# Another order of the block products in a fast matrix product on one core

## The chip, the cores and the metric

The kernel runs on one core of a Trainium2 chip. The metric is the time of the whole kernel on the device, in microseconds (us), as the median of several runs. One execution was also profiled; instructions in it are timed in nanoseconds.

## The reference

The input x has 8 batches of 512 rows of 1024 numbers, all in float32. The reference is a transformer layer with a normalization before and after each half:

```python
x = x + layernorm(attention(layernorm(x)))     # Wq, Wk, Wv, Wo, 16 heads of 64, rotary, causal
x = x + layernorm(ffn(layernorm(x)))           # x @ weight.T + bias, plus a LoRA term of rank 16
```

The LoRA term is `(x @ A.T) @ B.T`, with one of three adapters by batch. What matters here are the three products of the normalized rows with a 1024x1024 matrix: by Wv (the values), by Wo (the output projection) and by the weight of the FFN.

## The kernel before

Each of these products is made by a Strassen-Winograd scheme, twice over: seven products in place of eight at the outer level (`GROUPS`, P1 to P7), and each of these again by seven at the inner level (`SUBS`). So one batch takes 7 x 7 = 49 inner products. A batch in one of the three matrices is a **sequence**; sequences are numbered -8 to -1 for Wv (the projection stage), 0 to 7 for Wo (the output stage) and 8 to 15 for the FFN. Between the projection and the output stage lies the stage of Wq, Wk and the attention, which has a structure of its own and is not changed.

The order of all work is written out by hand. Time is counted in **ticks**: a tick is one inner product on TensorE (PE), two matmuls of 128x128 by 128x256, which in float32 are four passes in the trace. A sequence has 49 ticks, `N2`; its groups follow the list `ORDER`, and in a group the seven inner products follow `SLOTS`: P6, P1, P3, P5, P4, P7, P2. P3 in that list belongs to the group before, so that its sum can be read in two steps. `at(tick, fn)` puts a piece of work of another engine, or a DMA, to a tick, `run` issues a tick's work after its matmuls, and each engine and the DMA queue of SP take their work in the order in which it was issued. So an engine that is late delays all that is queued behind.

**Inner sums.** `product` adds the inner products in PSUM under four names, a, b, c and d. The drains (`drain`, one tick after their product) read them: after P1 ScalarE (ACT) copies a into p1 and VectorE (DVE) makes u2 = p1 + b; after P7 DVE makes p1 + b, then the quarter p1 + c (1, 1), then p1 + d (1, 0); after P2 ACT copies a, after P3 DVE makes u2 + c. A sum's bank can't be written before its last reader has read it: P3 adds to the c sum that the drain of P7 has just read.

**Outer sums.** A group's four quarters form a tile in SBUF: A, c11, c21, c22, U or c12 by group; A holds P1 and later P3. The result blocks are sums of such tiles. `COMBINE` lists them with their ticks and engines: on DVE one operation of 128x1024, on GpSimd (POOL) two of 128x512. With the order of before, the result blocks are finished by seven combines, most of them at ticks 45 to 52, the last three ticks in the next sequence. In the last sequence (15) the order was already `LAST`, with combines of its own.

**Operands.** The right operands are blocks R11, R21, R12, R22 of the rows and the sums T1 = R12 - R11, T2 = R22 - T1, T4 = R21 - T2, T3 = R22 - R12 (in R12's place). P1 uses R11, P2 R21, P3 R22, P4 T4, P5 T1, P6 T2, P7 T3. They are made during the sequence before (T1 from tick 38, T2 from 45, T4 from 52, T3 from 63, where ticks over 48 lie in the sequence that uses them), by DVE and POOL in the projection and FFN, by POOL alone in the output stage (line 275). They live in seven buffers, which change hands by `next_roles`: a block is loaded into the buffer whose group is done. The left operands (weights and their sums) stay for a whole stage; `plan_left` loads those of the FFN one by one during sequences 7 and 8.

**Other work in the same queues.** In the projection, DVE makes the statistics of the next batch (line 400), ACT normalizes it (420), PE transposes it (454). In the output and FFN stages the finished rows of a sequence are treated from tick 55 on in four parts: statistics on DVE, normalization on ACT, addition of the input on POOL (1124), and in the output stage statistics and a transposition on DVE again (1133), with loads and stores on SP.

The PSUM of the projection stage held one bank for a, two for b, two for c, one for d and two for transposes; from the output stage on a has two. That is all eight.

Of the kernel before, what the change touches and what calls it, by code (L numbers as in the profile page):

```python
# [58 lines left out]
    "P7": ("S3", "T3", "c12"),  # L59
}  # L60

ORDER = ["P1", "P2", "P4", "P5", "P7", "P6", "P3"]
LAST = ["P1", "P6", "P5", "P7", "P2", "P4", "P3"]
SUB = 256


# [12 lines left out]
ACCS = {"a": 1, "b": 2, "c": 2, "d": 1}  # L79
# [54 lines left out]
def sandwich_kernel(  # L134
# [139 lines left out]
        for c in (slice(0, 2), slice(2, 4), slice(4, 7))[part]:  # L274
            eng.tensor_tensor(RX[q, n][:, c], RX[q, x][:, c], RX[q, y][:, c], op=ALU.subtract)  # L275

    def next_roles():

        old = dict(role)
        for new, was in (("R11", "R11"), ("R21", "R21"), ("R12", "T4"), ("R22", "T1"),  # L280
                         ("T1", "R12"), ("T2", "T2"), ("T4", "R22")):
            role[new] = old[was]

    def open_c(q, tag):
# [10 lines left out]
    class Group:  # L295
# [9 lines left out]
        def product(self, p):  # L305
            l, r, a = SUBS[p]
            first = a not in self.acc
            if first:
                self.acc[a] = env["acc"].tile(
                    [P, SUB], F32, tag=a, bufs=2 if a == "a" and self.q >= 0 else ACCS[a], name=f"acc{a}_{self.name}"  # L310
                )
            acc = self.acc[a]
            left, right = self.W[self.L], RX[self.q, self.R][:, SLOT_R[r]]
            for k in range(2):
                stays = right[:, k, :] if self.q < B else by_blocks(right, k)
                if self.q < 0:
# [3 lines left out]
                nc.tensor.matmul(  # L320
                    acc, lhsT=stays, rhs=moving,
                    start=(first and k == 0), stop=True, skip_group_check=True,
                )
# [15 lines left out]
        def drain(self, p):  # L339

            acc, t = self.acc, self.t
            add = lambda out, x, a: nc.vector.tensor_tensor(out, acc[a], x, op=ALU.add)
            if p == "P1":
                env["u2"].reverse()
                for n, pool in (("p1", env["p1"]), ("u2", env["u2"][0])):
                    t[n] = pool.tile([P, SUB], F32, tag=n, name=f"{n}_{self.name}")
                nc.scalar.copy(t["p1"], acc["a"])
                add(t["u2"], t["p1"], "b")
            elif p == "P7":
                add(t["p1"], t["p1"], "b")  # L350
                add(self.dest(1, 1), t["p1"], "c")
                add(self.dest(1, 0), t["p1"], "d")
            elif p == "P2":
                nc.scalar.copy(self.dest(0, 0), acc["a"])
            elif p == "P3":
                add(self.dest(0, 1), t["u2"], "c")

    def combine(q, out, x, y, eng):
# [1 line left out]
            eng.tensor_tensor(C[q, out][:, j], C[q, x][:, j], C[q, y][:, j], op=ALU.add)  # L360


    COMBINE = (
        (18, nc.vector, "c11", "c11", "A"), (38, nc.gpsimd, "c21", "c21", "c12"),
        (45, nc.vector, "U", "U", "A"), (46, nc.vector, "c22", "c22", "U"),
        (47, nc.gpsimd, "c21", "c21", "U"), (48, nc.vector, "c12", "c12", "c22"),
        (52, nc.vector, "c22", "c22", "A"),
    )

    def products(q0, count, order, first=0):  # L370

# [100 lines left out]

    def plan_x(b, base):

        at(base + 10, next_roles)
        for t in range(NT):
            at(max(0, base - 12) + t, lambda t=t: load_x(b, t))
            k = (4, 5, 17, 19)[t]
            for m in range(4):
                at(base + k + m, lambda t=t, m=m: stats_x(b, t, m))  # L480
            at(base + k + 4, lambda t=t: norm_x(b, t))
        for n, k in (("R11", 11), ("R21", 18), ("R12", 25), ("R22", 32)):
            g, h = int(n[1]) - 1, int(n[2]) - 1
            for c in range(2):
                t = 2 * h + c
                at(base + k + c, lambda t=t, g=g: transpose_x(b, t, g), "pe")
                at(base + k + c, lambda pt, t=t, g=g: keep_x(b, t, g, pt), "post")
            at(base + k + 3, lambda n=n: sub_right(b - B, n, pool))
        for n, k in (("T1", 38), ("T2", 45), ("T4", 52), ("T3", 63)):
            eng = dve if n in ("T1", "T3") else pool  # L490
            for m in range(3):
                at(
                    base + k + (m if eng is dve else 0),
                    lambda n=n, m=m, eng=eng: sum_right(gvp, b - B, n, eng, slice(m, m + 1)),
                )
        for n, k in (
            ("R11", 18), ("R21", 25), ("R22", 40), ("T1", 44), ("T2", 54), ("T4", 60), ("T3", 69)
        ):
            at(base + k, lambda n=n: store_operand(b, n))

# [41 lines left out]
    for b in range(B):  # L542
        base = b * N2
        if b + 1 < B:
            plan_x(b + 1, base)
        for k, *op in COMBINE:
            at(base + k, lambda b=b, op=op: combine(b - B, *op[1:], op[0]))
        for k, tag, half, h in ((22, "c11", 0, 0), (53, "c21", 1, 0), (54, "c12", 1, 1), (57, "c22", 0, 1)):
            at(base + k, lambda b=b, tag=tag, half=half, h=h: store_v(b, tag, half, h))


# [337 lines left out]
    products(-B, B, lambda q: ORDER)  # L889
    psum.close()  # L890
    operands.close()
    late = {k - (B * N2 + 4): events[k] for k in sorted(events)}
# [88 lines left out]
    def first_product(n):  # L981
        nonlocal cur, before
        m, p = divmod(n, NP)
        if p == 0:
            L, R, tag = GROUPS[ORDER[m]]

            def mm(acc, p, first):
                l, r, _ = PRODUCTS[p]
                for k in range(2):
                    nc.tensor.matmul(  # L990
                        acc, lhsT=RX[0, R][:, SLOT_R[r], k, :],
                        rhs=LW["wo"][L][:, 4 * k : 4 * k + 4, SLOT_L[l], :],
                        start=(first and k == 0), stop=True, skip_group_check=True,
                    )

            def dest(i, j):
                if (0, tag) not in C:
                    open_c(0, tag)
                return C[0, tag][:, j, ts(i, SUB)]

            before, cur = cur, Product(nc, ps_p, tl, [P, SUB], f"0_{ORDER[m]}", mm, dest)
        cur.product(p)
        if p:
            cur.drain(p)
# [3 lines left out]
    for u in range(UQ + 1):  # L1008
# [15 lines left out]
        else:  # L1024
# [19 lines left out]
            at(base + 57, next_roles)  # L1044
# [21 lines left out]
    with ExitStack() as a:  # L1066
# [37 lines left out]

        def halves(q, t):
            h, j = divmod(t, 2)
            tags = (("c11", "c21"), ("c12", "c22") if q + 1 == NQ else ("c22", "c12"))[h]
            return [C[q, tag][:, j, :] for tag in tags]

        row = {}  # L1110
# [56 lines left out]
        def plan_right(q, base):  # L1167

            if q > 1:
                at(base + 6, next_roles)  # L1170
# [96 lines left out]
        for q in range(NQ):  # L1267
# [2 lines left out]
                plan_right(q + 1, base)  # L1270
            if q == B - 1:
                plan_left(base)
            dve, pool = nc.vector, nc.gpsimd
            for k, e, res, l, r in (
                (18, dve, "c11", "c11", "A"), (38, pool, "c21", "c21", "c12"), (45, dve, "U", "U", "A"),
                (46, dve, "c22", "c22", "U"), (47, pool, "c21", "c21", "U"),
                (48, dve, "c12", "c12", "c22"), (52, dve, "c22", "c22", "A"),
            ) if q + 1 < NQ else (
                (18, dve, "U", "U", "A"), (31, dve, "c12", "c12", "U"), (33, dve, "U", "U", "c22"),
                (34, pool, "c22", "c22", "c12"), (39, pool, "c11", "c11", "A"),  # L1280
                (45, dve, "c21", "c21", "c12"),
            ):
# [6 lines left out]
        products(0, NQ, lambda q: ORDER if q + 1 < NQ else LAST, AHEAD)  # L1289
        run_rest()  # L1290
    for pool in (wop2, tl, cl, gp, wop):
        pool.release()
# [105 lines left out]
```

## Time and profile before

| | us |
|---|---|
| median of 3 runs | 2468.2 (2465.58 to 2468.6) |
| profiled execution | 2470.53 |
| its span in the trace | 2468.4 |
| TensorE busy | 2356.1 (95%) |
| VectorE busy | 1790.1 (73%) |
| GpSimd busy | 1535.8 (62%) |

The first matmul of the projection starts 13 us after the start of the span, the last ends at about 429; the output stage proper begins at 1676, the FFN at 2024, and the last matmul ends at 2455. Lines of groups and waits name an engine, an operation or tile, the source line and, behind an arrow, what was read or what ended a wait. A wait is idle time of an engine between two of its instructions; three numbers behind it are the total, the count and the longest. The timeline has start, duration, engine, line, operation, out<-in and count; in brackets stands the idle time before it and who ended it.

### The profile page before, as it was taken

Reading aid. Unit: us, or ns where it says so; the run is one execution under the profiler, and the core shown is the slowest. Engines: PE = TensorE matmul, PEld = TensorE weight load, DVE = VectorE, ACT = ScalarE, POOL = GpSimd, SP = SyncE. Lnnn points to the kernel's source line nnn. Section 1 sums busy time; section 2 is a strip of 40 time slices with the busy share of each in tenths; the row PEclk is TensorE's granted clock in tenths of the full one; section 3 lists DMA queues with packets and bytes.
Section 4 is the critical chain, followed back from the end, with each engine's and each line's share of the span. In section 5 each row is a group of like instructions: output and inputs, shape, how many; then the busy total and the mean of one; then the engine's idle time right before and its main releaser. Section 6 shows DMA issues by size and latency. Waiting matters only on the chain.

```text
span 2468.4 us, 37185 instructions
## 1 busy us (share of the span) xinstructions
PE 2356.1 (95%) x11936; PEld 1858.0 (75%) x11936; DVE 1790.1 (73%) x3946; ACT 1045.4 (42%) x2650; POOL 1535.8 (62%) x1139
## 2 busy tenths in 40 slices
PE   6999999999999999999999999899999988999997
PEld 4887887886677777777777776558888867888886
DVE  8777767485857759577595866776899888776676
ACT  3323331025555555555555566652434433222223
POOL 4878875204363553735646364776887886777874
PEclk8999999999999999999999999899999999999999
DMA  7697787998899897989889897467777788545443
GB/s 264 196 302 247 245 269 230 353 304 265 269 298 291 248 340 239 312 297 292 314 259 341 265 303 245 135 230 261 241 213 233 216 261 246 136 144 148 139 122 119
DMA packets 506016, 606.47 MB, mean 246 GB/s; under 512 B 197600, under 2 KB 344032, under 8 KB 503264
## 3 DMA queue, kind: packets, MB, share of 16 engines
q1 hardware_dynamic: 504288, 598.87, 76.7%
q0 software_dynamic: 1536, 5.24, 0.7%
q8 instruction: 96, 1.57, 0.3%
q14 instruction: 96, 0.79, 0.1%
HBM read 371.20 MB, written 199.23 MB: 231 GB/s over the span
## 4 chain that ended last, share of the span: by engine, by line
PE 65%; DVE 6%; DMA 5%; POOL 2%; ACT 2%; issue 1%; SPq 1%; ACTq 0%; DVEq 0%; POOLq 0%
PE accb_q_P L641 7%; PE acca_q_P L641 7%; PE accc_q_P L641 7%; PE accc_P L320 6%; PE accb_P L320 6%; PE acca_P L320 6%; PE s L753 6%; PE po L835 6%; PE ptp L814 5%; PE accd_q_P L641 3%; PE accd_P L320 3%; DMA wo_d<-wc_wo 1%; DVE U L360 1%; ACT pr L784 1%; DMA attn<-opt 1%
## 5 line engine op out<-in xcount | busy, mean ns | idle before, releaser
L784 ACT ACTIVATE pr<-pr,nm 128x128 f32<-128x128 f32 (+3 forms) x512 | 281.0, 550 | 188.4 <-DVE nm L774 188.2
L800 ACT ACTIVATE pr<-pr,rs 128x128 f32<-128x128 f32 x470 | 231.0, 550 | 109.4 <-DVE rs L792 109.3
L774 DVE CUSTOM_DVE_ANT_0 pr<-s,mask 128x128 f32<-128x128 f32 (+3 forms) x512 | 224.2, 484 | 43.1 <-PE s L753 41.1
L641 PE MATMUL acca_q_P<-xs,ls 128*128 128x256 f32 x896 | 217.3, 385 | 0.8 <-DMA ls<-wqk 0.8
L641 PE MATMUL accc_q_P<-xs,ls 128*128 128x256 f32 x896 | 217.1, 385 | 0.0
L641 PE MATMUL accb_q_P<-xs,ls 128*128 128x256 f32 x896 | 216.3, 384 | 0.8 <-DVE u_q_P L117 0.8
L1124 POOL TENSOR_TENSOR c<-c,row 128x512 f32<-128x512 f32 x120 | 161.8, 1357 | 88.4 <-ACT c L420 73.2
L641 PEld LDWEIGHTS acca_q_P<-xs,ls 128*128 128x128 f32 x896 | 165.3, 190 | 49.9 <-issue 19.4
L641 PEld LDWEIGHTS accc_q_P<-xs,ls 128*128 128x128 f32 x896 | 165.3, 190 | 48.2 <-issue 20.2
L641 PEld LDWEIGHTS accb_q_P<-xs,ls 128*128 128x128 f32 x896 | 165.4, 190 | 44.9 <-issue 6.6
L753 PE MATMUL s<-qk 64*128 64x128 f32 (+3 forms) x1024 | 192.5, 472 | 4.4 <-DVE nm L774 4.2
L814 PE MATMUL ptp<-ident,pr 128*128 128x128 f32 x1280 | 178.7, 278 | 12.8 <-DVE nm L774 5.9
L814 PEld LDWEIGHTS ptp<-ident,pr 128*128 128x128 f32 x1280 | 147.6, 142 | 44.8 <-ACT pr L800 15.9
L275 POOL TENSOR_TENSOR T<-R,T 128x512 f32<-128x512 f32 (+1 forms) x96 | 171.3, 1812 | 14.2 <-PE accc_P L320 9.6
L567 POOL TENSOR_TENSOR wc_g<-wc_g 128x256 f32<-128x256 f32 (+1 forms) x120 | 127.0, 1077 | 79.6 <-DMA wc_g<-in_wqk_dram 76.3
L835 PE MATMUL po<-pT,v 128*64 128x512 f32 (+3 forms) x1024 | 157.6, 446 | 8.2 <-ACT pT L829 6.1
L835 PEld LDWEIGHTS po<-pT,v 128*64 128x64 f32 x1024 | 72.8, 138 | 100.1 <-issue 66.2
L684 POOL TENSOR_TENSOR B_q<-B_q,m 128x1024 f32<-128x1024 f32 x14 | 33.1, 2368 | 175.7 <-DVE B_q L681 175.7
L641 PE MATMUL accd_q_P<-xs,ls 128*128 128x256 f32 x448 | 108.8, 386 | 0.4 <-DVE p_q_P L117 0.4
L829 DVE COPY pT<-ptp 128x384 f32<-128x384 f32 (+1 forms) x132 | 80.4, 614 | 39.3 <-PE ptp L814 39.2
L753 PEld LDWEIGHTS s<-qk 64*128 64x128 f32 x1024 | 73.1, 186 | 44.7 <-issue 28.7
L567 POOL TENSOR_TENSOR wc_wo<-wc_wo 128x256 f32<-128x256 f32 (+1 forms) x64 | 66.0, 1049 | 64.2 <-DMA wc_wo<-in_wo_dram 50.8
(1120 smaller groups left out, 5750.6 us busy)
## 6 DMA issues: line engine op xcount, KB each, us to landing
ls<-wqk SPq DMA_DIRECT2D x392, 256.0 KB, 5.3
xs<-xop SPq DMA_DIRECT2D x392, 256.0 KB, 5.4
R<-attn SPq DMA_DIRECT2D x32, 896.0 KB, 6.4
wqk<-wc_g SPq DMA_DIRECT2D x16, 1568.0 KB, 9.4
x<-in_x_dram SPq DMA_DIRECT2D x32, 512.0 KB, 9.7
v<-vd SPq DMA_DIRECT2D x64, 256.0 KB, 5.4
attn<-ops SPq DMA_DIRECT2D x16, 1024.0 KB, 7.7
row<-in_x_dram SPq DMA_DIRECT2D x32, 512.0 KB, 5.4
```

Source lines behind the costliest of these rows:

```text
L275: eng.tensor_tensor(RX[q, n][:, c], RX[q, x][:, c], RX[q, y][:, c], op=ALU.subtract)
L320: nc.tensor.matmul(acc, lhsT=stays, rhs=moving, start=(first and k == 0), stop=True, skip_group_check=True,)
L567: eng.tensor_tensor(out, x, y, op=op)
L641: nc.tensor.matmul(acc[:, :, w, :], lhsT=ls[:, k, w, :], rhs=xs_[:, :, k, :], start=(first and w == 0 and k == 0), stop=True, skip_group_c ...
L753: nc.tensor.matmul(ps[:, j, at : at + L], lhsT=qT[r, qb], rhs=kT[r, : qb + 1], start=True, stop=True,)
L774: nc.vector.tensor_tensor_reduce(out=v[:, j, :], in0=self.ps[qb][:, j, :], in1=work2["mask"][:, S - L :], scale=-1.0 / HD**0.5, scalar=3.0e38,
L784: nc.scalar.activation(v[:, j, :], v[:, j, :], AF.Exp, bias=nm[:, j : j + 1], scale=-1.0, accum_out=sm[:, j : j + 1],)
L800: nc.scalar.mul(v, v, rs[:, j : j + 1])
L814: nc.tensor.transpose(pt[:, n, :], self.pr[qb][:, j, ts(kb, P)], ident)
L829: copy(self.pT[j][:, : qb + 1, ts(qb, P)], self.pt[j][:, : qb + 1, :])
L835: nc.tensor.matmul(po[j * HD : (j + 1) * HD, kb * P :], lhsT=self.v[:, kb, ts(j, HD)], rhs=self.pT[j][:, kb, kb * P :], start=(kb == 0), s ...
L1124: nc.gpsimd.tensor_tensor(c, c, row[q, t][:, ts(h, HALF)], op=ALU.add)
```

## The change

All sequences but the first of a stage (-8 and 0) take their groups in the order P1, P6, P5, P7, P2, P4, P3, which only the last sequence had before. With this order a result tile is summed soon after each group, so the combines stand at ticks 17, 31, 35, 36, 39, 45 and 52. The last one writes c12 from A and U, so the second half of the output takes its two tiles in the other order (`halves`). As the operands come free in another order, `next_roles` has a second table, and the loads of the FFN's weights follow the groups. T3 of the projection is made at tick 59 in place of 63, and the stores of the values (`store_v`) and of T3 move to where these are ready.

In PSUM the c and d sums become two halves of one bank, in two banks by turns, and a gets two banks in all stages. The quarter that reads d is now made before the one that reads c.

```diff
-ORDER = ["P1", "P2", "P4", "P5", "P7", "P6", "P3"]
-LAST = ["P1", "P6", "P5", "P7", "P2", "P4", "P3"]
+FIRST = ["P1", "P2", "P4", "P5", "P7", "P6", "P3"]
+ORDER = ["P1", "P6", "P5", "P7", "P2", "P4", "P3"]
...
-    def next_roles():
+    def next_roles(q):
...
-        for new, was in (("R11", "R11"), ("R21", "R21"), ("R12", "T4"), ("R22", "T1"),
-                         ("T1", "R12"), ("T2", "T2"), ("T4", "R22")):
+        for new, was in (
+            ("R11", "R11"), ("R21", "R21"), ("R12", "T4"), ("R22", "T1"), ("T1", "R12"), ("T2", "T2"), ("T4", "R22"),
+        ) if q - 1 in (-B, 0) else (
+            ("R11", "R11"), ("R21", "T2"), ("R12", "T1"), ("R22", "R12"), ("T1", "R21"), ("T2", "T4"), ("T4", "R22"),
+        ):
...
-            if first:
-                self.acc[a] = env["acc"].tile(
-                    [P, SUB], F32, tag=a, bufs=2 if a == "a" and self.q >= 0 else ACCS[a], name=f"acc{a}_{self.name}"
-                )
+            if a in "ab" and first:
+                self.acc[a] = env["acc"].tile([P, SUB], F32, tag=a, bufs=2, name=f"acc{a}_{self.name}")
+            elif a == "c" and first:
+                both = env["acc"].tile([P, 2, SUB], F32, tag="c", bufs=2, name=f"accc_{self.name}")
+                self.acc["c"], self.acc["d"] = both[:, 0], both[:, 1]
...
                 add(t["p1"], t["p1"], "b")
+                add(self.dest(1, 0), t["p1"], "d")
                 add(self.dest(1, 1), t["p1"], "c")
-                add(self.dest(1, 0), t["p1"], "d")
...
-    COMBINE = (
-        (18, nc.vector, "c11", "c11", "A"), (38, nc.gpsimd, "c21", "c21", "c12"),
-        (45, nc.vector, "U", "U", "A"), (46, nc.vector, "c22", "c22", "U"),
-        (47, nc.gpsimd, "c21", "c21", "U"), (48, nc.vector, "c12", "c12", "c22"),
-        (52, nc.vector, "c22", "c22", "A"),
-    )
+        first = (
+            (17, dve, "U", "U", "A"), (31, dve, "c12", "c12", "U"), (35, dve, "U", "U", "c22"),
+            (36, pool, "c22", "c22", "c12"), (39, pool, "c11", "c11", "A"), (45, dve, "c21", "c21", "c12"),
+        )
+        return first if last else (*first, (52, dve, "c12", "A", "U"))
...
-        for n, k in (("T1", 38), ("T2", 45), ("T4", 52), ("T3", 63)):
+        for n, k in (("T1", 38), ("T2", 45), ("T4", 52), ("T3", 59)):
...
-        for k, tag, half, h in ((22, "c11", 0, 0), (53, "c21", 1, 0), (54, "c12", 1, 1), (57, "c22", 0, 1)):
+        for k, tag, half, h in (
+            (41, "c22", 1, 1), (44, "c11", 0, 0), (48, "c21", 1, 0), (55, "c12", 0, 1),
+        ) if b else (
+            (22, "c11", 0, 0), (53, "c21", 1, 0), (54, "c12", 1, 1), (57, "c22", 0, 1),
+        ):
...
-            for n, k in zip(("L11", "L12", "L22", "S1", "S3", "S2", "S4"), (10, 22, 34, 46, 56, 64, 72)):
+            for n, k in zip(("L11", "S2", "S1", "S3", "L12", "L22", "S4"), (10, 22, 34, 46, 56, 64, 72)):
```

More of the change, by code (lines that the diff above doesn't have):

```diff
@@ L78 @@
 QK = {"P1": "A", "P2": "B", "P6": "D", "P7": "E", "P4": "F", "P5": "D", "P3": "E"}
-ACCS = {"a": 1, "b": 2, "c": 2, "d": 1}
 SLOT_L = {"L11": 0, "L12": 1, "S3": 2, "L22": 3, "S1": 4, "S2": 5, "S4": 6}
@@ L360, in combine, with order_of, combines @@
             eng.tensor_tensor(C[q, out][:, j], C[q, x][:, j], C[q, y][:, j], op=ALU.add)
-    COMBINE = (
-        (18, nc.vector, "c11", "c11", "A"), (38, nc.gpsimd, "c21", "c21", "c12"),
-        (45, nc.vector, "U", "U", "A"), (46, nc.vector, "c22", "c22", "U"),
-        (47, nc.gpsimd, "c21", "c21", "U"), (48, nc.vector, "c12", "c12", "c22"),
-        (52, nc.vector, "c22", "c22", "A"),
-    )
+    def order_of(q):
+        return FIRST if q in (-B, 0) else ORDER
+    def combines(q, last=False):
+        dve, pool = nc.vector, nc.gpsimd
+        if q in (-B, 0):
+            return (
+                (18, dve, "c11", "c11", "A"), (38, pool, "c21", "c21", "c12"), (45, dve, "U", "U", "A"),
+                (46, dve, "c22", "c22", "U"), (47, pool, "c21", "c21", "U"),
+                (48, dve, "c12", "c12", "c22"), (52, dve, "c22", "c22", "A"),
+            )
+        first = (
+            (17, dve, "U", "U", "A"), (31, dve, "c12", "c12", "U"), (35, dve, "U", "U", "c22"),
+            (36, pool, "c22", "c22", "c12"), (39, pool, "c11", "c11", "A"), (45, dve, "c21", "c21", "c12"),
+        )
+        return first if last else (*first, (52, dve, "c12", "A", "U"))
     def products(q0, count, order, first=0):
@@ L473, in plan_x @@
     def plan_x(b, base):
-        at(base + 10, next_roles)
+        at(base + 10, lambda: next_roles(b - B))
         for t in range(NT):
@@ L496, in plan_x @@
         for n, k in (
-            ("R11", 18), ("R21", 25), ("R22", 40), ("T1", 44), ("T2", 54), ("T4", 60), ("T3", 69)
+            ("R11", 18), ("R21", 25), ("R22", 40), ("T1", 44), ("T2", 54), ("T4", 60), ("T3", 67)
         ):
@@ L545, in sandwich_kernel @@
             plan_x(b + 1, base)
-        for k, *op in COMBINE:
+        for k, *op in combines(b - B):
             at(base + k, lambda b=b, op=op: combine(b - B, *op[1:], op[0]))
-        for k, tag, half, h in ((22, "c11", 0, 0), (53, "c21", 1, 0), (54, "c12", 1, 1), (57, "c22", 0, 1)):
+        for k, tag, half, h in (
[3 more added lines that the diff above has]
+        ):
             at(base + k, lambda b=b, tag=tag, half=half, h=h: store_v(b, tag, half, h))
@@ L887, in plan @@
                     at(base + last + k, lambda m=m: self.sum(m))
-    products(-B, B, lambda q: ORDER)
+    products(-B, B, order_of)
     psum.close()
@@ L984, in first_product @@
         if p == 0:
-            L, R, tag = GROUPS[ORDER[m]]
+            L, R, tag = GROUPS[FIRST[m]]
             def mm(acc, p, first):
@@ L999, in dest @@
                 return C[0, tag][:, j, ts(i, SUB)]
-            before, cur = cur, Product(nc, ps_p, tl, [P, SUB], f"0_{ORDER[m]}", mm, dest)
+            before, cur = cur, Product(nc, ps_p, tl, [P, SUB], f"0_{FIRST[m]}", mm, dest)
         cur.product(p)
@@ L1043, in sandwich_kernel @@
                     at(base + k + m, lambda n=n, m=m: sum_right(gp, 0, n, nc.gpsimd, slice(m, m + 1)))
-            at(base + 57, next_roles)
+            at(base + 57, lambda: next_roles(1))
             for n in ("R12", "R11", "R21"):
@@ L1106, in halves @@
             h, j = divmod(t, 2)
-            tags = (("c11", "c21"), ("c12", "c22") if q + 1 == NQ else ("c22", "c12"))[h]
+            tags = (("c11", "c21"), ("c12", "c22") if q else ("c22", "c12"))[h]
             return [C[q, tag][:, j, :] for tag in tags]
@@ L1169, in plan_right @@
             if q > 1:
-                at(base + 6, next_roles)
+                at(base + 6, lambda: next_roles(q))
             for n, k in (("R11", 10), ("R21", 17), ("R12", 24), ("R22", 31)):
@@ L1272, in sandwich_kernel @@
                 plan_left(base)
[L1273 to L1282, printed above, removed]
+            for k, e, res, l, r in combines(q, q + 1 == NQ):
                 if base + k >= AHEAD:
@@ L1288, in sandwich_kernel @@
                 plan_last(q, base)
-        products(0, NQ, lambda q: ORDER if q + 1 < NQ else LAST, AHEAD)
+        products(0, NQ, order_of, AHEAD)
         run_rest()
```

## The prediction

> **What bounds the kernel now.** I read the page first, then the waits of PE stage by stage, then the timelines of DVE and POOL around the longest of them. The page:
>
> ```profile
> span 2468.4 us, 37185 instructions
> PE 2356.1 (95%) x11936; PEld 1858.0 (75%) x11936; DVE 1790.1 (73%) x3946; ACT 1045.4 (42%) x2650; POOL 1535.8 (62%) x1139
> ```
>
> TensorE sets the time and the change leaves its matmuls alone, so only its waits can be won. One tick is four 128x256 matmul passes at 0.216 us from start to start, 0.865 us; 49 ticks are 42.4 us. A pass lasts 0.38 us and overlaps the next, so a wait costs its idle time plus 0.16 us. From first matmul to first matmul in the timeline, projection sequences -6 to -2 take 49.1 us each (46.3 without their waits; transposes are the rest), output sequences 2 to 6 take 46.2, 44.7, 44.4, 44.6 and 46.2, and FFN sequences 10 to 14 take 51.7. PE's waits in three windows (134 to 380, 1700 to 1976, 1976 to 2100 us):
>
> ```profile
> PE ptx L454 <- ACT x L420: 3.7, 15, 0.4
> PE acca_-6_P L320 <- ACT A_-6_1100 L354: 0.8, 1, 0.8
> ...
> PE accc_-4_P L320 <- DVE A_-4_2162 L342: 0.3, 1, 0.3
> ...
> PE accc_P L320 <- DVE A L342: 11.0, 6, 1.9
> PE accb_P L320 <- POOL T L275: 1.6, 1, 1.6
> ...
> PE accc_P L320 <- DVE A L342: 7.6, 2, 4.2
> PE ph L1153 <- DMA R<-x1t: 5.0, 4, 2.2
> PE accb_P L320 <- DVE u_P L342: 3.7, 2, 2.1
> ```
>
> From 2100 to 2452 us there are none. The usual wait is P3 of a sequence's last group (tick 51) for DVE's read of its c sum. Why DVE is late there, in the timeline of DVE at the seam of output sequences 3 and 4 (start, us, line, tiles):
>
> ```profile
> 1833.49 1.76 DVE L360 TENSOR_TENSOR U<-U,A 128x1024 f32<-128x1024 f32 x1
> 1835.28 2.17 DVE L360 TENSOR_TENSOR c<-c,U 128x1024 f32<-128x1024 f32 x1
> 1837.38 0.41 DVE L342 TENSOR_TENSOR p_P<-accb_P,p_P 128x256 f32<-128x256 f32 x1
> 1837.82 0.42 DVE L342 TENSOR_TENSOR A<-accc_P,p_P 128x256 f32<-128x256 f32 x1
> 1838.16 0.41 DVE L342 TENSOR_TENSOR A<-accd_P,p_P 128x256 f32<-128x256 f32 x1
> 1838.49 1.21 DVE L360 TENSOR_TENSOR c<-c,c 128x1024 f32<-128x1024 f32 x1
> ```
>
> Two combines stand ahead of the drain of P7, whose product was ready at 1834.4. And POOL in the same place:
>
> ```profile
> 1824.96 2.50 POOL L1124 TENSOR_TENSOR c<-c,row 128x512 f32<-128x512 f32 x2 [5.44 <-DMA row<-in_x_dram]
> 1827.42 4.29 POOL L275 TENSOR_TENSOR T<-R,R 128x512 f32<-128x512 f32 x3
> 1831.66 2.51 POOL L360 TENSOR_TENSOR c<-c,c 128x512 f32<-128x512 f32 x2
> 1834.12 7.28 POOL L275 TENSOR_TENSOR T<-R,T 128x512 f32<-128x512 f32 x3
> ```
>
> **The change, part by part.** Combines stay five on DVE and two pairs on POOL, 1.2 us each on DVE when POOL is quiet and 1.5 to 2.3 beside it (4.1 twice). They move: on DVE from ticks 18, 45, 46, 48, 52 to 17, 31, 35, 45, 52; on POOL from 38 and 47 to 36 and 39.
>
> *Second bank for a in the projection.* P1's wait for ScalarE's copy goes: 0.75 + 0.16 = 0.91 a sequence. Nothing else queued on PE needs that copy before the next group. Bounds 0.9 and, if the next wait simply grows, 0.3.
>
> *Projection seam.* Ticks 45 to 52 held 1.93 + 2.17 + 1.71 + 1.51 = 7.3 us of combines and keep two, about 3.7. So the P3 wait goes (0.47), and the statistics of x behind it start about 1.1 us earlier against PE, which cuts the three transpose waits (0.36, 0.32, 0.55) to some 0.4 in all; T3, moved from tick 63 to 59, falls into DVE gaps of 1.3 and 1.5 us and takes away 0.21 at tick 23. The combines at 31 and 35 lie in DVE gaps of 1.8 and 3.0 us. Back comes 0.2 at tick 44, where T1 already made DVE 1.0 us late. Together 0.91 + 0.47 + 0.83 + 0.21 - 0.2 = 2.2, of 2.8 there are: 11 for sequences -6 to -2.
>
> *Other projection sequences.* Sequence -7 has 2.1 of such waits, keeps 0.3, and gets a new one: T2 is now wanted in group 1, at 92.4, and POOL finished it at 93.2: 0.8. Gain 1.0. Sequence -1 has 4.7 of waits on DVE and loses one combine and half a burst ahead of them: 2.5. Sequence -8 keeps its order: 0.5. The stage: 15 (9 to 19).
>
> *Seam of output sequences 0 and 1.* P4's wait for T4 (1.56 + 0.16) goes, since P4 now comes in group 5. T2 ended at 1707.1 and P6 now wants it at tick 7, 1706.1: 1.0 comes. Gain 0.7.
>
> *Six output seams, before sequences 2 to 7.* They cost 11.0 + 6 x 0.16 = 12.0, and behind two of them (1748 and 1928 us) eight and some more passes start 0.43 apart instead of 0.22, 3.4 in all: 15.4. With sequence 3 as the example: the combine at tick 31 lands at 1822.6, where DVE had no gap, so P7's drain of tick 34 starts 1.6 late. A drain may be late by 2.26 - 1.25 = 1.0, since P3 follows P7 by three ticks and now waits for three reads instead of two (c is read last): 0.5 of wait. The combine at tick 35 ends at 1827.7 to 1828.5, and DVE's gaps up to tick 44 are 0.7, 0.1 and 0.3, so the next two groups add 0.1 to 0.9 and 0 to 1.0. POOL's sum into c22 must wait for that same combine (it overwrites what DVE reads), and T1, c11 and T2 are queued behind it: 1828 + 2.5 + 4.3 + 2.5 + 4.3 to 6.2 = 1841.6 to 1843.5, against P6 at 1841.1 plus what PE has lost by then. The second write of A (tick 48) waits for c11 too, at about 1837, where DVE arrives anyway. The two chains run side by side, so I take the later: 1.6 a seam (0.6 to 3). Six make 9.6; of the slow passes half stay, 1.7. Gain 15.4 - 11.3 = 4.1 (+13 to -6).
>
> Trainium skill, TensorE: Matmul & The Clock Gate, Part 1, has the clock halved after an idle window of about 3.4 us. The trace has it behind a wait of 1.92 us, and not behind one of 1.94. By the rule no output seam would ever pay the 3.4, and shortening the waits would win 1.7 less; I go by the rows.
>
> *Sequences 8 and 9.* Waits for DVE of 4.4 + 2.2 and 3.5 + 1.8, then slow passes of some 3.5. Here U took 4.13 beside POOL's T2, and the combine that replaces it stands in the same place; the tick 35 combine pushes u by 1.2. One combine fewer in the burst leaves about 0.5 each: gain 1 (+9 to -3). The DMA waits of ph stay.
>
> Trainium skill, SBUF — State Buffer, section Who interferes with whom: a DVE operation with two SBUF inputs and a GpSimd one lock each other out for a whole instruction. The 4.13 agrees, the 1.21 at 1838.49 under POOL's T does not: there POOL paid. By the rule alone each combine moved to ticks 31 and 35 could pay for a GpSimd operation of 1.27, up to 2.5 a seam more than the 1.2 each from quiet places; the forecast's 0.6 to 3 a seam takes in both.
>
> *FFN sequences 10 to 15.* DVE has gaps of 2.7 and 2.2 us where the new combines fall, and POOL finishes T2 about 3 us ahead: nothing. At the very end P3 waits for one more read: +0.4. Loads keep their distance from their use, because the order of roles and of the last weights moves with the groups.
>
> Sum: 15 + 0.7 + 4.1 + 1 - 0.4 = 20.4. The profiled execution took 2470.5; 2450.1, and on the median of the runs (2468.2) 2448.
>
> **The rivals.** *All seams clear* (0.15): combines find POOL quiet, 1.2 us each, and PE's own small waits give DVE time; then the output seams give 13 and sequences 8 and 9 give 6: 2434. For it: POOL has a gap of 5.4 us before 1825. Against: DVE is busy 40 of 44 us there.
>
> *The projection gives half* (0.18): the normalization of x, or transfers (79% busy there), is next behind the copy, and 0.91 turns into a longer transpose wait: 2456.
>
> *POOL's chain decides* (0.09, slower): T2 has 28 ticks less, and c22 and c11 go ahead of it. If its parts all run at the rows' crowded 2.25 each instead of 1.27, c22, T1, c11 and T2 take 22 us instead of 14; P6 then waits 8 us at each of six seams, 48 against 11 allowed for, and the kernel takes 2485. From 5.3 us a seam on (the 1.9 allowed for, and a sixth of 20.4) all that is won is lost. Against: fewer combines on DVE now fall on T2.
>
> *Nothing moves* (0.03): the waits only change their names, 2468.
>
> **How the numbers follow.** The forecast has 0.55: 2448. Its own bounds are 2436 to 2458; to leave out no more than 2 in 10 the range takes the half projection and the near part of the clear seams: 2432 to 2461. A change under 0.2% (4.9 us) can't be told from none. Faster 0.86, same 0.05, slower 0.09.
>
> **What would show it.** Right: no PE wait on ACT A in the projection and 46.9 us a sequence there; at the output seams P3 waits at ticks 37, 44 or 51 of under 1 us, and P6 at tick 7 for POOL's T; FFN sequences at 51.7. Wrong: PE waiting over 3 us on POOL's T, DVE waiting for POOL at the second A, or transposes waiting longer on ACT x.

## The result, and the profile after

The changed kernel is slower. Its median is 2486.3 us (four runs, 2482.8 to 2492.3) beside 2466.9 of the kernel before on the same chip, a ratio of 1.0082 with a 95% interval of 1.0059 to 1.0104. On a second occasion it took 2482.1 beside 2469.5, 1.0055 (1.0038 to 1.0072). The forecast was 2448 (2432 to 2461): neither the sign nor the range held.

The profiled execution took 2482.8, the fastest of its four. The first lines of its page:

```profile
span 2481.0 us, 37063 instructions
...
PE 2356.8 (95%) x11936; PEld 1858.0 (75%) x11936; DVE 1813.0 (73%) x3946; ACT 1046.7 (42%) x2650; POOL 1519.2 (61%) x1139
```

TensorE's busy time is the same as before (2356.1), so the 12.6 us that the span grew are waits. By stages, from the timeline of PE:

| stretch | before | after | difference | forecast |
|---|---|---|---|---|
| start to the first matmul of the stage of Wq and Wk | 429.6 | 441.8 | +12.3 | -15 |
| from there to sequence 1 | 1270.5 | 1265.2 | -5.3 | 0 |
| sequences 1 to 7 | 324.3 | 323.6 | -0.7 | -4.8 |
| sequence 8 to the end of the span | 444.0 | 450.3 | +6.3 | -0.6 |

On the second occasion the profiled execution was the slowest of its four (2486.5). There the same four rows differ from before by +12.0, -2.2, -3.5 and +9.9: the projection's loss repeats, while what the other stages gain or lose varies by some 3 us.

The projection's loss repeats in every sequence, too: most take 50.45 us from first matmul to first matmul, against 49.1 before and 46.9 forecast; -7 and -1 lose 2.4 and 2.5. The waits of PE in the after kernel, in one projection sequence (238 to 288 us; total, count, longest):

```profile
PE accc_-4_P L323 <- DVE c_-4_2094 L345: 1.7, 1, 1.7
PE accc_-4_P L323 <- DVE U_-4_1881 L345: 1.1, 1, 1.1
PE accc_-4_P L323 <- DVE A_-4_1811 L345: 0.5, 1, 0.5
PE ptx L468 <- ACT x L434: 0.2, 1, 0.2
```

The wait for ScalarE's copy and the seam's wait are gone as forecast. In their place P3 waits at ticks 44, 16 and 9 for DVE's read of the c sum. DVE's timeline in the after kernel (start, us, line, tiles, shapes, count) shows what stands ahead of the drain of P7 (p, then the two quarters) that P3 waits for at tick 16 and at tick 44:

```profile
250.29 4.15 DVE L274 TENSOR_TENSOR R_-4_1623<-R_-4_1669,R_-4_1623 128x512 f32<-128x512 f32 x3
254.37 0.41 DVE L345 TENSOR_TENSOR p_-4_P<-accb_-4_P,p_-4_P 128x256 f32<-128x256 f32 x1
254.81 0.75 DVE L345 TENSOR_TENSOR U_-4_1881<-accc_-4_P,p_-4_P 128x256 f32<-128x256 f32 x2
...
277.90 5.28 DVE L274 TENSOR_TENSOR T_-3_2074<-R_-3_1986,R_-3_1866 128x512 f32<-128x512 f32 x3
283.10 0.41 DVE L345 TENSOR_TENSOR p_-4_P<-accb_-4_P,p_-4_P 128x256 f32<-128x256 f32 x1
283.55 0.76 DVE L345 TENSOR_TENSOR c_-4_2094<-accc_-4_P,p_-4_P 128x256 f32<-128x256 f32 x2
```

The first group is T3 (in R12's place), the second T1, each three operations without a gap. POOL, in the after kernel, beside them:

```profile
246.42 9.01 POOL L585 TENSOR_TENSOR wc_g<-wc_g 128x256 f32<-128x256 f32 x8
...
277.75 2.94 POOL L363 TENSOR_TENSOR c_-4_1938<-c_-4_1938,c_-4_2000 128x512 f32<-128x512 f32 x2
280.65 3.65 POOL L363 TENSOR_TENSOR c_-4_2045<-c_-4_2045,A_-4_1811 128x512 f32<-128x512 f32 x2
```

Both pairs of POOL, c22 and c11, now lie under T1. Before, only one pair did, and T1's three parts took 3.35 us together; they take 5.28 now. T1 on DVE and the pair on POOL, before:

```profile
272.53 3.35 DVE L275 TENSOR_TENSOR T_-3_2104<-R_-3_2019,R_-3_1894 128x512 f32<-128x512 f32 x3
```
```profile
271.51 2.95 POOL L360 TENSOR_TENSOR c_-4_1968<-c_-4_1968,c_-4_2078 128x512 f32<-128x512 f32 x2
```

In the output stage the waits of PE (1700 to 1976 us, after kernel) are:

```profile
PE accc_P L323 <- DVE A L345: 5.1, 5, 1.0
PE accb_P L323 <- DVE u_P L345: 2.7, 6, 0.9
PE accc_P L323 <- DVE c L345: 1.2, 6, 0.2
PE accb_P L323 <- POOL T L274: 0.9, 1, 0.9
```

The first line is P3 at tick 51 (1.0 at each seam), the second P7 at tick 40 for DVE's sum u2 (0.35 at most seams), the third P3 at tick 37 (0.20), the last P6 of sequence 1 for T2. The single waits of 1.9 and the slow passes behind two of them are gone, but the 5.1 has a new owner, on DVE and then on POOL at the same seam:

```profile
1841.20 0.42 DVE L345 TENSOR_TENSOR p_P<-accb_P,p_P 128x256 f32<-128x256 f32 x1
1843.68 0.76 DVE L345 TENSOR_TENSOR A<-accc_P,p_P 128x256 f32<-128x256 f32 x2 [2.06 <-POOL c L363]
```
```profile
1840.08 3.57 POOL L363 TENSOR_TENSOR c<-c,A 128x512 f32<-128x512 f32 x2
```

DVE stands idle for 2.06 us because POOL's c11 += A still reads the A that DVE is to overwrite. In the FFN, DVE and then POOL at the seam of sequences 10 and 11:

```profile
2201.87 4.64 DVE L363 TENSOR_TENSOR c<-c,c 128x1024 f32<-128x1024 f32 x1
```
```profile
2201.15 4.26 POOL L274 TENSOR_TENSOR T<-R,T 128x512 f32<-128x512 f32 x3
```

The combine c21 += c12 takes 1.2 us alone. Here it ends at 2206.5, 1.1 us behind the end of POOL's run of three operations of T2, as if it had got its turn only then.

### The profile page after: what moved, and what is told of

Read it like the earlier page. It is cut to its first block, busy times and chain, and to the rows that moved or that the text cites. A ratio compares the mean times of both kernels' runs of the same rounds, so it can differ in the third digit from the quotient of the medians.

```text
span 2481.0 us, 37063 instructions
## 1 busy us (share of the span) xinstructions
PE 2356.8 (95%) x11936; PEld 1858.0 (75%) x11936; DVE 1813.0 (73%) x3946; ACT 1046.7 (42%) x2650; POOL 1519.2 (61%) x1139
## 4 chain that ended last, share of the span: by engine, by line
PE 71%; DVE 17%; POOL 3%; DMA 3%; ACT 2%; issue 2%; SPq 1%; DVEq 0%; ACTq 0%; POOLq 0%
PE accc_P L323 8%; PE accb_q_P L659 7%; PE acca_q_P L659 7%; PE accc_q_P L659 7%; PE s L771 6%; PE po L853 6%; PE ptp L832 5%; PE accb_P L323 5%; PE acca_P L323 5%; PE accd_q_P L659 4%; DVE c L363 1%; DMA R<-x1t 1%; POOL T L274 1%; DVE T L274 1%; POOL c L363 1%
## 5 line engine op out<-in xcount | busy, mean ns | idle before, releaser
L659 PEld LDWEIGHTS accc_q_P<-xs,ls 128*128 128x128 f32 x896 | 166.6, 191 | 48.2 <-issue 23.9
L274 POOL TENSOR_TENSOR T<-R,T 128x512 f32<-128x512 f32 (+1 forms) x96 | 153.3, 1626 | 31.3 <-PE accc_P L323 26.6
L262 POOL TENSOR_TENSOR R<-R 128x256 f32<-128x256 f32 x96 | 92.4, 963 | 46.3 <-DMA R<-x1t 38.1
```

The source lines that it names most:

```text
L262: eng.tensor_tensor(t[:, out], t[:, x], t[:, y], op=ALU.subtract)
L659: nc.tensor.matmul(acc[:, :, w, :], lhsT=ls[:, k, w, :], rhs=xs_[:, :, k, :], start=(first and w == 0 and k == 0), stop=True, skip_group_c ...
```

## The experiments

Two theories. **Order**: DVE is late because of what now stands ahead of its drains, and beside what on POOL. **Banks**: DVE is late, or P3 waits longer, because c and d share a bank: P3 has to wait for three reads of DVE (b, d, c) in place of two (b, c). The ratios are to the kernel before, run on the same chip and occasion; its medians there are 2469.3 for experiments 1 to 4, 2468.0 for 5 to 8, 2469.5 for 9 and 2468.6 for 10.

**1. The order alone.** After, with the sums in PSUM as before:

```diff
-            if a in "ab" and first: ...   # and c, d as halves of one bank
+            if first:
+                self.acc[a] = env["acc"].tile([P, SUB], F32, tag=a, bufs=2 if a == "a" and self.q >= 0 else ACCS[a], ...)
...
-                add(self.dest(1, 0), t["p1"], "d")
                 add(self.dest(1, 1), t["p1"], "c")
+                add(self.dest(1, 0), t["p1"], "d")
```

> The new order of groups and combines alone; the PSUM sums stand as before (c and d in banks of their own, one bank for a in the projection, the quarter from c ahead of the one from d). In the changed kernel P3 waits in each projection sequence at ticks 9, 16 and 44 (0.47, 1.15 to 1.68 and 1.66 us) for DVE's read of the c sum. Theory 'order': DVE is late there because of where T1, T3 and the combines now stand; then these waits stay, each smaller by at most the one read of 0.41 that P3 need not wait for, and ScalarE's copy of a is waited for again (0.75 a sequence): the two nearly cancel, the kernel takes 2476 to 2486 and the first matmul of the stage of Wq and Wk starts 9 us or more later than before. Theory 'banks': the waits come from the third read that the shared bank adds; then the kernel takes 2467 or less and the projection sequences return to 49.1.

Measured: 2475.4, ratio 1.0025 (1.0011 to 1.0039). A projection sequence takes 49.8. Waits of PE from 230 to 284 us in this kernel:

```profile
PE accc_-4_P L323 <- DVE c_-4_2128 L345: 1.3, 1, 1.3
PE accc_-5_P L323 <- DVE c_-5_1758 L345: 1.3, 1, 1.3
PE accc_-4_P L323 <- DVE U_-4_1911 L345: 0.8, 1, 0.8
```

The waits at ticks 44 and 16 stay, each 0.33 smaller (1.33 for 1.66, 0.82 for 1.15 in the trace). That is just below the range of "order" and above that of "banks": each has a part. The expectation of "order" was wrong in two points: the stage of Wq and Wk starts some 6 us later than before, not 9 or more, and the wait for ScalarE's copy is 0.25, not 0.75.

**2. The banks alone.** The other half of the change on the kernel before:

```diff
-                self.acc[a] = env["acc"].tile([P, SUB], F32, tag=a, bufs=2 if a == "a" and self.q >= 0 else ACCS[a], ...)
+            if a in "ab" and first: ...   # two banks for a; c and d halves of one bank
...
+                add(self.dest(1, 0), t["p1"], "d")
                 add(self.dest(1, 1), t["p1"], "c")
-                add(self.dest(1, 0), t["p1"], "d")
```

> The PSUM part alone: c and d in one bank, a in two, the quarter from d made first; order, combines and T's as before. Theory 'order': the second bank for a takes away 0.91 a projection sequence, the third read costs up to 0.41 at the one place a sequence where DVE is late already (the seam); the kernel takes 2460 to 2468. Theory 'banks': P3 waits of some 1.2 to 1.6 appear at ticks 9, 16 or 44 of the projection sequences as in the changed kernel, and the kernel takes 2478 or more.

Measured: 2474.3, ratio 1.0020 (1.0006 to 1.0035), and a projection sequence of 49.11, to 0.01 us that of before. PE's waits (134 to 380 us) show why the second bank for a brought nothing:

```profile
PE accc_-4_P L321 <- DVE A_-4_1811 L343: 0.6, 1, 0.6
...
PE accc_-4_P L321 <- DVE A_-4_2127 L343: 0.6, 1, 0.6
...
PE accc_-4_P L321 <- DVE c_-4_1937 L343: 0.4, 1, 0.4
```

The first is tick 9, one tick behind the old wait of 0.75 for ScalarE at tick 8: 0.64 of it comes back as a wait for DVE. The other two stood in the kernel before with 0.30 (the seam) and 0.04 (tick 23); the third read adds 0.34 and 0.33. "Order" missed the time by 6 us. It counted the third read once a sequence and the second bank as a gain; and in the profile sequence -1 takes 2.1 more than before and the FFN 2.9, which no theory had. "Banks" was wrong in expecting the big waits here. Neither half alone does to a projection sequence what both do: the order costs 0.69, the banks 0.00, both together 1.35.

**3. T3 back at tick 63.**

```diff
-        for n, k in (("T1", 38), ("T2", 45), ("T4", 52), ("T3", 59)):
+        for n, k in (("T1", 38), ("T2", 45), ("T4", 52), ("T3", 63)):
...
-            ... ("T3", 67)
+            ... ("T3", 69)
```

(The second pair is the store of T3.)

> The changed kernel with the projection's T3 back at tick 63 (its store at 69). T3's three operations of 0.80, 1.62 and 1.89 us now stand on DVE right ahead of the drain of P7 that P3 waits for at tick 16 (1.15 to 1.68 us). If that placement makes the drain late, the wait at tick 16 falls under 0.5 in sequences -6 to -2, a sequence takes 49.3 to 49.9 instead of 50.5, and the kernel gains 4 to 8 us on the changed one; the waits at ticks 9 and 44 stay. If the lateness comes from the third read or from something carried over from the seam, the wait moves to tick 23 and the time stays within 2 us of the changed kernel.

Measured: 2478.5, ratio 1.0036 (1.0025 to 1.0048), 4 to 8 us less than the changed kernel's two medians. A sequence takes 50.2, less of a gain than expected, and the waits (230 to 284 us) say that both answers hold:

```profile
PE accc_-5_P L323 <- DVE c_-5_1731 L345: 1.7, 1, 1.7
PE accc_-4_P L323 <- DVE c_-4_2094 L345: 1.7, 1, 1.7
PE accc_-4_P L323 <- DVE c_-4_1937 L345: 0.6, 1, 0.6
PE accc_-4_P L323 <- DVE A_-4_1811 L345: 0.5, 1, 0.5
```

Tick 16 is clear, but half of its wait stands at tick 23 now; ticks 44 and 9 are untouched. The stage of Wq and Wk starts 6.9 us earlier than in the changed kernel, and 4.7 of that lie in sequence -1, which takes 45.7 (50.4 in the changed kernel, 47.9 before).

**4. c11 on DVE, c21 on POOL, in all stages** (but for the last sequence; the stores of the values follow).

```diff
-            (39, pool, "c11", "c11", "A"), (45, dve, "c21", "c21", "c12"),
+            (45, dve, "c11", "c11", "A"), (45, pool, "c21", "c21", "c12"),
...
```

> The changed kernel with two combines exchanged between engines (all sequences but the last): c11 on DVE at tick 45, c21 on POOL at tick 45; the stores of the values follow. In the changed kernel T1's three parts on DVE take 1.67, 1.75 and 2.02 beside POOL's c22 and c11 (before: 0.81, 1.75, 0.94), DVE idles 2.06 us at the second write of A because POOL's c11 still reads A, and c21 takes 4.1 to 4.6 beside POOL's T2. Theory 'order': with c11 off POOL there, the tick 44 wait of the projection (1.66) falls under 0.9, the output seams lose the wait at tick 51 (1.0), and the kernel takes 2462 to 2476. Theory 'banks': DVE's load is the same, the third read still stands, and the time stays within 4 us of the changed kernel.

Measured: 2485.3, ratio 1.0070 (1.0042 to 1.0097): no gain, and this is not "banks" being right. With c11 gone from beside it T1 takes 4.21 us on DVE instead of 5.28, and the tick 44 wait, the second line, falls from 1.66 to 0.58:

```profile
279.95 4.21 DVE L274 TENSOR_TENSOR T_-3_2074<-R_-3_1986,R_-3_1866 128x512 f32<-128x512 f32 x3
```
```profile
PE accc_-4_P L323 <- DVE c_-4_2092 L345: 0.6, 1, 0.6
```

Sequences 8 and 9 took 113.7 instead of 120.8, with 10 to 14 at 51.7 but for one of 53.2. But a new wait ate it, on DVE in the projection:

```profile
243.34 2.27 DVE L363 TENSOR_TENSOR c_-5_1637<-A_-5_1765,U_-5_1518 128x1024 f32<-128x1024 f32 x1 [1.31 <-POOL c_-5_1729 L363]
```

DVE's c12 = A + U overwrites the c12 that POOL's c21 still reads; DVE waits 1.31 for it with the statistics and the next drain behind, and P3 waits 2.04 at tick 9 of each sequence. In the output stage the same wait of DVE is 2.0 a sequence. One line of PE's waits, then one of DVE's, from 1700 to 1976 us in this kernel:

```profile
PE accc_P L323 <- DVE A L345: 9.3, 5, 1.9
```
```profile
DVE c L363 <- POOL c L363: 10.2, 5, 2.0
```

P3 waits 1.86 at tick 9 here, with slow passes behind three of these waits, and sequences 1 to 7 take 332.7 instead of 323.6. That undoes most of the 11 us that the part from sequence 8 on gains.

**5. T1 of the projection on POOL, c11 on DVE at tick 39.**

```diff
-            (39, pool, "c11", "c11", "A"),
+            (39, dve if q < 0 else pool, "c11", "c11", "A"),
...
-            eng = dve if n in ("T1", "T3") else pool
+            eng = dve if n == "T3" else pool
```

> The changed kernel with two pieces of the projection exchanged between engines: T1 (three parts, now 1.67 + 1.75 + 2.02 us on DVE at ticks 38 to 40) on POOL, and c11 (two parts, 3.7 us on POOL) on DVE at tick 39. Nothing else moves. Theory 'T1 beside POOL's sums makes the drain of tick 41 late': DVE has about 1.5 to 2 us there instead of 5.4, the wait of P3 at tick 44 (1.66 a sequence) falls under 0.3, sequences -6 to -2 take 48.7 to 49.3 instead of 50.5, and the first matmul of the stage of Wq and Wk starts 7 to 11 us earlier than in the changed kernel (441.8). The kernel gains 4 to 11. Rival 'the loss is carried along': the lateness comes from the seam and the sequence keeps its 50.5, the wait moving to tick 2 or 9.

Measured: 2474.1, ratio 1.0028 (1.0017 to 1.0038), 8 to 12 less than the changed kernel. A sequence takes 48.2, and the waits from 230 to 284 us have lost tick 44:

```profile
PE accc_-4_P L323 <- DVE U_-4_1878 L345: 1.2, 1, 1.2
PE ptx L468 <- ACT x L434: 0.2, 1, 0.2
```

Tick 9 fell as well (0.11 left). The stage of Wq and Wk starts at 430.8, 11.0 us earlier than in the changed kernel. One sequence lost: -7 waits 2.7 us at its start, because T1 for it now queues on POOL among the sums of the first sequence, which has the old order, and a combine of DVE waits 3.0 for one of these sums.

**6. The exchange of experiment 4 in the FFN alone.**

```diff
+        if q >= B and not last:
+            first = (*first[:4], (45, dve, "c11", "c11", "A"), (45, pool, "c21", "c21", "c12"))
```

> The changed kernel with two combines of the FFN alone exchanged: c11 on DVE and c21 on POOL, both at tick 45. In the changed kernel c21 on DVE takes 4.1 to 4.6 us beside POOL's T2 there. Where all stages had this exchange, the part from the start of sequence 8 to the last matmul took 424.9 us, against 435.9 in the changed kernel and 429.2 before. Theory 'c21 beside T2': the part takes 424 to 427 here too, sequences 10 to 14 take 51.7 and the kernel gains 7 to 11 on the changed one. Rival: 424.9 came from starting later (2041 instead of 2031), with loads that were ahead; then the part takes 431 or more.

Measured: 2478.3, ratio 1.0039 (1.0024 to 1.0054), 4 to 8 less than the changed kernel. Four of the sequences 10 to 14 take 51.70 to 52.11 (52.10 to 53.97 in the changed kernel). On DVE the combine that now stands in the place of the 4.64, and then POOL's sum, in this kernel:

```profile
2200.38 1.21 DVE L363 TENSOR_TENSOR c<-c,A 128x1024 f32<-128x1024 f32 x1
```
```profile
2200.53 2.19 POOL L363 TENSOR_TENSOR c<-c,c 128x512 f32<-128x512 f32 x1 [2.16 <-DVE c L345]
```

The whole part took 431.4, which the rival had: what experiment 4 won more lay in sequences 8 and 9, whose first waits differ from execution to execution (118.2 here).

**7. The old projection, the new order from sequence 1 on**, with the PSUM of before and the exchange in the FFN:

```diff
-        return FIRST if q in (-B, 0) else ORDER
+        return FIRST if q <= 0 else ORDER
```

(and the same condition in `combines`, `next_roles` and the stores of the values; T3 at 63).

> The projection as before in order, combines and PSUM; the new order from sequence 1 on, with the PSUM sums of before and the exchange of c11 and c21 in the FFN. Expected from the parts: the projection's sequences take 49.1 and the stage ends at 429 to 430; the output seams gain 3 as with the order alone, the FFN 3 to 4. Theory 'the loss of the change is in the projection and the FFN's c21': 2460 to 2464, 5 to 9 less than before. Rival: the output stage's gain is an accident of the late start there; then 2466 or more.

Measured: 2464.8, ratio 0.9993 (0.9980 to 1.0005), between the two ranges. In the one profile the output stage gained 2.2 (3 expected) and the FFN 3.4; the median is 3.2 below that of the kernel before and can't be told from no change. So the profile has the order win a little in the later stages, with the old banks and the exchange, and the medians don't show it. With the old order and banks the last product of the projection starts at 428.1 (427.6 before).

**8. A mix**: experiments 1, 5 and 6 together, and T3 at ticks 59, 60 and 63 with its store at 69.

```diff
-                    base + k + (m if eng is dve else 0),
+                    base + k + ((0, 1, 4)[m] if n == "T3" else m if eng is dve else 0),
```

> The new order everywhere with the PSUM sums of before, T1 of the projection on POOL and c11 on DVE, T3 in parts at ticks 59, 60 and 63 so that only 2.4 us of it stand ahead of the drain of P7, and the exchange of c11 and c21 in the FFN. If the waits at ticks 16 and 44 (0.82 and 1.33 us with the order alone) are DVE's queue and nothing else, both fall under 0.2, a projection sequence takes 47.3 to 47.9 instead of 49.8 (49.1 before) and the stage ends at 419 to 423; with 3 from the output seams and 4 from the FFN the kernel takes 2450 to 2460. Rival 'POOL is next': POOL, busy 77% there before, gets 1.6 us more a sequence, T2 or T4 come late, and the sequences stay over 49.

Measured: 2465.4, ratio 0.9992 (0.9983 to 1.0002). Most sequences take 46.8 to 47.5, but -7 takes 56.6 and -4 50.3. Beside the start of -7 (as in experiment 5), PE's waits from 120 to 280 us name ScalarE's copies of the a sum:

```profile
PE acca_-7_P L323 <- ACT c_-7_968 L357: 3.1, 1, 3.1
PE acca_-4_P L323 <- ACT c_-4_2075 L357: 2.1, 1, 2.1
```

ScalarE itself waited for the store of T3, whose buffer it was to fill with the next R22.

**9. The mix with both mended.**

```diff
-            eng = dve if n == "T3" else pool
+            eng = dve if n == "T3" or (n == "T1" and b == 1) else pool
...
-            ... ("T3", 69)
+            ... ("T3", 67)
```

> The mix of before with two corrections. In the mix, sequence -7 took 56.6 us, because T1 for it on POOL stood among the sums of the first sequence (T2 came 3 us late), and in sequences -7 and -4 ScalarE waited at tick 35 for the store of T3, which had been put behind a 512 KB load at tick 69. Now T1 for sequence -7 is on DVE again and the store at tick 67. If these are the two causes, sequence -7 takes 48 to 50 and all from -6 to -2 46.8 to 47.6, the projection ends some 9 us earlier than in the mix (428), and the kernel takes 2452 to 2460. Rival: the stage of Wq and Wk, whose length went from 1267 to 1275 as the projection got shorter, takes the gain back; then the projection is shorter by 9 and the time stays at 2463 or more.

Measured: 2454.3, ratio 0.9948 (0.9931 to 0.9966), the fastest version: 15 us less than before and 28 less than the changed kernel on the same occasion. PE's waits from 134 to 380 us, five projection sequences, are all here:

```profile
PE ptx L470 <- ACT x L436: 1.7, 10, 0.2
PE acca_-6_P L323 <- ACT A_-6_1099 L357: 0.7, 1, 0.7
```

A sequence takes 46.80, the last product of the projection starts at 419.6 (427.6 before, 440.1 after), and in sequences -6 to -2 no wait on DVE is left. Sequence -1 keeps one: P3 waits 4.4 us at tick 9, since DVE has idled 6.2 us for the load of a block of the next stage's weights (wc_g) that stands ahead of the drain in its queue.

**10. The same with the PSUM part of the change**, the hunk of experiment 2.

> The second mix (2454.3 us) with the change's PSUM part added: c and d in one bank, a in two, the quarter from d made first. In the second mix no P3 wait is left in projection sequences -5 to -2 (46.80 us each) and none at the output seams (44.34). Theory 'the third read costs only where DVE is late': the slack of P3 falls from 1.38 to 0.97 us everywhere, but only places where a drain of P7 starts over 0.97 late pay, up to 0.41 each; projection sequences take 46.8 to 47.6, output sequences 44.3 to 44.8, and the kernel takes 2454 to 2462. Rival 'the shared bank costs in itself': each of the seven P3 of a sequence pays and the sequences take 1.5 us or more longer, 2480 or more. Third: the second bank for a brings what was forecast, and the kernel gets faster, 2445 to 2450.

Measured: 2459.1, ratio 0.9961 (0.9945 to 0.9978). The first theory holds: projection sequences of 46.8 (one of 47.4), output sequences of 44.68 in place of 44.34. The expectation was wrong to say that the mix had no wait at the output seams; it has two of 0.7 each. Here, from 1740 to 1976 us:

```profile
PE accc_P L324 <- DVE A L346: 5.1, 5, 1.0
PE accb_P L324 <- DVE u_P L346: 1.7, 5, 0.4
PE accc_P L324 <- DVE c L346: 1.0, 5, 0.2
```

They are those of the changed kernel. Where DVE is late, the third read costs its 0.33; where not, nothing. The second bank for a brings little: in the profile it removes two waits for ScalarE (0.5 in sequence -7, 0.7 in -6), -5 gets a new P3 wait of 0.6, and the projection ends 1.6 us earlier; the output stage takes 2.4 us longer. The two intervals overlap, so that the part costs time here is shown by the output sequences, not by the medians.

The eleventh run was the changed kernel once more:

> The changed kernel once more, beside the runs of before of the same chip, so that the versions built on it are compared with more than four of its runs. Every theory expects 2482 to 2490.

Its time is given at the top; it has the same 50.47 and 44.68 a sequence.

## Why the prediction was wrong, point by point

The forecast for a projection sequence was 46.9 and 50.45 came. The waits for ScalarE, at the seam and for the transposes went as forecast. The 3.55 us between forecast and result are three terms of the sum, each with the 0.16 that the prediction adds to a wait's idle time:

- **"Back comes 0.2 at tick 44, where T1 already made DVE 1.0 us late."** It was 1.66 + 0.16 = 1.82, so the term was 1.62 too small. The duration of T1 was taken over from a trace in which one POOL pair lay beside it; the change puts two there, and T1 goes from 3.35 to 5.28 us. Experiments 4 and 5 show it: without c11 beside T1 the wait is 0.58, without T1 on DVE it is gone. This is the largest failed step.
- **"T3, moved from tick 63 to 59, falls into DVE gaps of 1.3 and 1.5 us."** T3 is one block of 4.15 us behind which a drain is queued, and two gaps of 2.8 together don't hold it. The 0.21 at tick 23 was won as forecast, but at tick 16 a wait of 1.15 + 0.16 = 1.31 came, for which the sum had nothing. Experiment 3 removes this wait and brings half of it back at tick 23, where three parts together are still one block.
- **"Nothing else queued on PE needs that copy before the next group": 0.91 a sequence.** The copy itself was not needed, but the next product on PE is P3, and that waits for DVE, which was nearly as late as ScalarE. Experiment 2 has 0.64 for 0.75, a gain of 0.1. In the changed kernel the next tick costs 0.47 + 0.16 = 0.63, which leaves 0.28 of the 0.91: the lower bound that the prediction gave (0.3, "if the next wait simply grows").

1.62 + 1.31 + 0.63 = 3.56. The third read, which the prediction priced at 0.5 for the output seams only, is part of the first two: 0.33 each.

**The other projection sequences.** -8, -7 and -1 were to gain 0.5, 1.0 and 2.5 and lost 0.7, 2.4 and 2.5, some 10 us of the 27 between the forecast of the stage and its result. In -7 the waits at ticks 16 and 44 stand as in the others (1.77 and 1.18), and P6's wait for T2, priced at 0.8, took 0.37. In -1 the combines were not what decided. P3 waits 1.66 at tick 9 and 3.57 at tick 16, with eight slow passes behind the second. T3 at its new tick stands there between DVE's sums of the next stage's weights (wc_g), ahead of the drain; DVE in the changed kernel:

```profile
403.11 3.42 DVE L274 TENSOR_TENSOR R_-1_2712<-R_-1_2758,R_-1_2712 128x512 f32<-128x512 f32 x2
406.45 1.54 DVE L585 TENSOR_TENSOR wc_g<-wc_g 128x448 f32<-128x448 f32 x1
```

With T3 back at 63 (experiment 3) both waits are gone and the sequence takes 45.7, 2.2 us less than before, where 2.5 were forecast. How much of this is T3, and how much the load of wc_g for which DVE idles ahead of tick 9, no run separates. What sequence -8 lost was not followed.

**The price of a wait** was low as well. Four passes behind a wait take 1.13 us in the timeline, others 1.03, so a wait costs its idle time plus 0.26 rather than 0.16. A projection sequence has about as many waits before as after, and there it cancels; at an output seam one wait became three.

**Output stage.** Most of the mechanisms named were right: P3 waits of about 1 us and less at ticks 37 and 51, and P6 of sequence 1 for T2 with 0.9 against 1.0. The wait expected at tick 44 did not come; P7 waits at tick 40 instead, for DVE's u2 behind the combine of tick 35. The second A waits for POOL's c11, and not at a time "where DVE arrives anyway": DVE idles 2.06 for it. Six seams were priced at 9.6; their waits are 5.1 + 1.0 (the sixth lies behind the window shown) + 2.7 + 1.2 = 10.0 of idle time, and there are 18 of them, each with its price. The slow passes, for which 1.7 was kept, went entirely. By the starts of the sequences the six seams gained 2.0 instead of 4.1: sequences 1 to 6 take 1.7 less, 0.7 of it at the seam of 0 and 1, and the sixth wait, in sequence 7, is 0.9 shorter. The rest of the shortfall lies at the end of sequence 7, where one wait of 3.9 stands, at a place that the prediction had counted with sequences 8 and 9. In the second profile it is missing, and the stage gains 3.5 of the 4.8 forecast.

**FFN.** The last sequence costs 0.3 more, as forecast (0.4), and 8 and 9 together 1.0 (forecast -1). But 10 to 14 cost 5.4 (5.9 in the second profile): "DVE has gaps of 2.7 and 2.2 us where the new combines fall" looked at ticks 31 and 35 and not at tick 45, where c21 keeps company with POOL's T2 and grows from 1.2 to 4.6. The prediction had seen the same in the kernel before (4.13 beside T2) and used it for sequences 8 and 9 only. Experiment 6 shows it.

**The rival that was slower** named POOL's chain, with P6 waiting 8 us a seam for T2. That did not happen; P6 waited once, 0.9. The kernel is slower by DVE's queue in the projection and at tick 45 of the FFN, for which the prediction had no case at all. So the chance of 0.09 on slower stood on the wrong mechanism.

**The stage of Wq and Wk**, with code that is not changed, took 1266 to 1275 us (from the last product of the projection to sequence 1) in the thirteen profiles, with no order that the changes explain; it gave 5.5 us in the first profile of the changed kernel, 2.4 in the second and 4 in experiment 9. That stays open.

**The slow passes.** In these traces passes 0.43 apart instead of 0.22 follow waits of 2.71 (experiment 5), 2.97 and 3.15 (experiment 8). Of six output seams of experiment 2 with waits of 2.24 to 2.26 one has eight such passes behind it. Waits of 2.04 (experiment 4), 2.11 (experiment 8), 3.02 (experiment 9) and, before the change, 2.68 had none. So the length of one wait does not decide it here. The Trainium skill, TensorE: Matmul & The Clock Gate, Part 1, sets the halved clock behind an idle window of about 3.4 us, which does not describe these rows.

## What to carry to other kernels

When work on one engine is moved, price each operation by what will lie beside it on the other engine at the new place, not by its duration at the old one: here T1 grew from 3.35 to 5.28 us and c21 from 1.2 to 4.6 without a line of them being changed. A gap in an engine's timeline holds a piece of work only if the whole block that is issued together fits ahead of the next drain; in the second mix two parts of T3 ahead of the drain and the third behind it cost no wait in sequences -6 to -2, where in the changed kernel three parts together cost one at either place tried. Before a buffer is doubled to take a wait away, ask what the very next instruction waits for: if that is an engine equally late, the wait only changes its name.

## What the runs showed of the hardware

DVE operations on SBUF tiles stretch by up to 3.4 us beside a run of POOL operations (4.64 against 1.21 for the same 128x1024 sum), and in the mended place it was POOL that paid, 2.19 us instead of 1.26 for a half. The 4.64 ends 1.1 us behind the last of three POOL operations, about the time that the sum takes alone, so here one DVE instruction seems to have lost to a whole run; the 4.13 before the change ends 1.1 us behind such a run as well. The Trainium skill, SBUF — State Buffer, section Who interferes with whom, has the pair of ports that the two share locked for a whole instruction, by the one that issues first; one instruction of POOL's run is 1.3 to 1.8 us, so by that alone the sum would have taken about 3 us at most, an estimate.

The Trainium skill, PSUM — Partial Sum Buffer, section PSUM bank collisions raise a hardware error, forbids two engines on one bank at a time. No run here shows it, and the other order of reads in the shared bank (c first, so that P3 would wait for two reads) was not tried for that reason.
